# Layer 1 of a two-layer gated attention kernel: a list of units with counts per step, and turns by block transposes and DMAs

## The chip, the core and the metric

The kernel runs on one core of one Trainium2 chip. The metric is the device time of one launch in microseconds. A core has TensorE (matmuls; PE in the profile), VectorE (DVE), ScalarE (ACT), GpSimd (POOL) and SyncE (SP), which here issues nearly all DMAs; all engines run at the same time and wait for each other by semaphores. SBUF holds 128 partitions; PSUM has eight banks of 128 x 512 float32.

## The reference

The input is 16 batches of 128 tokens of width 512, with 128 context rows of width 128 per batch. Two layers each do attention to the context and a feed-forward part, both behind a layer norm and added through a tanh gate. All is float32. Layer 0 has attention with 16 heads through latents of width 64, and a feed-forward part with two of eight low-rank adapters per token. The change is in layer 1:

```python
# attention, 16 heads of 32
qp = q @ Wq.T                                   # q = layernorm(x)
k, v = jnp.split(latent_kv @ Wkv_expand.T, 2, axis=-1)
scores = jnp.einsum('bhqd,bhkd->bhqk', qh, kh) * inv_sqrt_d   # causal
attn = jax.nn.softmax(scores, axis=-1)
out = jnp.einsum('bhqk,bhkd->bhqd', attn, vh) ... @ Wout.T
# feed-forward: a mixture of 8 low-rank maps per token
h = relu(x @ W1 + b1)
alpha = softmax(h @ W2 + b2)                    # 8 shares per token
vx = jnp.einsum('krd,bsd->bskr', V, x)
out = jnp.einsum('bsk,bskd->bsd', alpha, jnp.einsum('kdr,bskr->bskd', U, vx))
```

## The kernel before

The 16 batches form four groups of four (`GB = 4`, `GT = 512` tokens). Projections run over the tokens of a whole group, attention over one batch. TensorE contracts over partitions, so the normalised rows (tokens on partitions) have to be turned (features on partitions) before a product. The kernel turns in two ways. `turned` (L1164) lets TensorE transpose four 128 x 128 blocks into PSUM, and `drain` (L1158) copies them out on VectorE or ScalarE. `standard` (L1198) has VectorE transpose 32 x 32 blocks in place, and `turn_all` (L1192) moves the blocks with 16 DMAs on SyncE, each of 32 partitions.

In layer 1, group `g` and batch `b` go through these steps:

- `load_latents`, `latents` (L1172, L1176): load the context of a group, turn it on TensorE through a "tr" PSUM tile, drain it to `kvT`, and start the next group's load. `keys(g, c)` (L1185) makes four tiles of keys.
- `standard`, `tokens` (L1218): normalise and turn a group's rows; `queries(g, c)` (L1222) makes four tiles of queries.
- `score(b)` (L1235): values and scores of a batch (two PSUM pools), then the softmax on VectorE, ScalarE and GpSimd, and block transposes into the only buffer `eb` (L1261). `carry(b)` (L1265) moves the lower blocks with ten DMAs to `late[:, 0]` or `eT_even`. `values(b)` (L1271) and `project(b)` (L1284) finish the attention; the residual and its moments run on VectorE.
- `ffn_normal`, `ffn_tokens` (L1300, L1312): normalise a group for the feed-forward part into `late[:, 1]` and turn it on TensorE. `hidden(g, c)`, `share_parts(g)`, `shares(g)` (L1318, L1334, L1347) make the shares of the eight maps and send them through DRAM to `late[:, 2]` or `late[:, 3]` by 4 and 8 DMAs. `ranks(g, c)` and `mixture(b)` (L1377, L1387) make the output, and `store` (L1400) sends it.

Tiles come from pools. The tag "xn" of `lnp` has two buffers for rows of 512; the tag "xnT" has one for a turned group; the tag "tr" has two PSUM banks, "mm" four and "acc" two. A new tile waits until the last reader of a buffer is done.

The order of work is set in two ways. On TensorE and SyncE the layer's instructions stay in program order (L164 to L177, `keep_in_program_order`). On VectorE, ScalarE and GpSimd a planner orders them at build time by its own estimates, with the program order as priority. At run time each engine goes through its own list in order.

The main loop (L1531) runs over steps `s` from 2 to 17. It does the values and projection of batch `b = s - 2` and the scores of batch `s`. Between them, `take` (L1436) pulls units from the list `fill`. Each entry has a step from which it may run and a cost (16 for most), and a running debt `owed` decides how many units a call pulls. `near[0]` tells `drain` to use VectorE only, right behind a score. Layer 0's last down products are mixed with the first queries, keys and scores ahead of the loop (L1500 to L1530).

Of the kernel before, what the change touches and what calls it, by code (L numbers as in the profile page):

```python
# [42 lines left out]
def kernel(  # L43
# [1132 lines left out]
    def latents(g):  # L1176
        tr = tr_tile(f"kv1tr_{g}")
        for i in range(GB):
            transpose(tr[:, ts(i, P)], kv[g][:, i, :], ident)
        kvT[g] = le.tile([P, GT], F32, tag="kvT", name=f"kv1T_{g}")  # L1180
        drain(kvT[g], tr)
        if g + 1 < NG:
            load_latents(g + 1)
# [34 lines left out]
    def tokens(g, xb):  # L1218
        xa[g] = lnp.tile([P, ND, GT], F32, tag="xnT", name=f"xnT_a1_{g}", bufs=1)
        turn_all(xa[g].rearrange("p c (i t) -> p (c i) t", i=GB), xb)  # L1220

    def queries(g, c):  # L1222
        q_ps = tr_tile(f"q1_ps{g}_{c}")
        for d in range(ND):
            matmul(
                q_ps, aqo_sb[:, d, ts(c, P)], xa[g][:, d, :],
                start=(d == 0), stop=(d == ND - 1),
            )
        q_c = le.tile([P, GT], F32, tag=f"q{c}", name=f"q1_{g}_{c}")
        drain(q_c, q_ps)  # L1230
        qs.setdefault(g, []).append(q_c)
# [68 lines left out]
    def ffn_normal(g):  # L1300
# [3 lines left out]
        nc.vector.reciprocal(rstdf[:, bs], rstdf[:, bs])  # L1304
        for i in range(GB):
            b = g * GB + i
            nc.vector.tensor_scalar(
                late[:, 1, 4 * i : 4 * i + 4].rearrange("p c t -> p (c t)"), xt[b],
                mvf[:, b, 0:1], rstdf[:, b : b + 1], ALU.subtract, ALU.mult,
            )  # L1310

    def ffn_tokens(g):  # L1312
        xf[g] = ap.tile([P, ND, GT], F32, tag="xf", name=f"xf_{g}", bufs=1)
        for i in range(GB):
            turned("f1", g * GB + i, late[:, 1, 4 * i : 4 * i + 4].rearrange(
                "p c t -> p (c t)"), xf[g])
# [30 lines left out]
    def shares(g):  # L1347
# [23 lines left out]
        avT[g] = late[:, 2 + g % 2].rearrange("p (c i) t -> p c i t", c=ND)  # L1371
# [5 lines left out]
    def ranks(g, c):  # L1377
        v_ps = (tr_tile if g < NG - 1 else mm_tile)(f"vx_ps{g}_{c}")
# [28 lines left out]
    def next_queries(g):  # L1407
        for c in range(ND):
            yield 16, lambda c=c: queries(g, c)

    def hiddens(g):
        for c in range(ND):
            yield 16, lambda c=c: hidden(g, c)
        yield 2, lambda: share_parts(g)

    def all_ranks(g):
        for c in range(ND):
            yield 16, lambda c=c: ranks(g, c)

    def mixtures(g, start, end):  # L1420
        for i in range(start, end):
            yield 16, lambda i=i: mixture(g * GB + i)

    def at(step, units):
        return [(step, n, u) for n, u in units]

    fill = at(AHEAD, next_queries(1)) + at(4.5, next_queries(2))
    fill += at(6, hiddens(0)) + at(7.5, next_queries(3))
    fill += at(8.5, all_ranks(0)) + at(8.5, mixtures(0, 0, 2))
    fill += at(10.5, hiddens(1)) + at(10.5, mixtures(0, 2, 4)) + at(11, all_ranks(1))  # L1430
    fill += at(11, mixtures(1, 0, 2))
    fill += at(14.5, hiddens(2)) + at(15, mixtures(1, 2, 4)) + at(16, all_ranks(2))
    fill += at(17, mixtures(2, 0, 1)) + at(NB + AHEAD, mixtures(2, 1, 2))
    owed = [0]

    def take(step, cost):  # L1436
        owed[0] += cost
        while owed[0] > 0:
            if not fill or fill[0][0] > step:
                owed[0] = 0  # L1440
                break
            _, n, unit = fill.pop(0)
            unit()
            owed[0] -= n
# [58 lines left out]
    for n in range(1, 3):  # L1503
        down(q, n)
    for c in range(ND):
        if c == 2:
            latents(0)
# [22 lines left out]
    standard(late[:, 1], 2, mv1, rstd1, "a1")  # L1530
    for s in range(AHEAD, NB + AHEAD):  # L1531
        b = s - AHEAD
        first, second, third = (0, 18, 14) if s < GB + AHEAD else (14, 28, 20)
        if b > GB and b % GB == 0:
            first, second = first + 16, second - 16
        values(b)
        settle()
        turn = s < NB and s % GB == 0
        if turn:
            latents(s // GB)  # L1540
        take(s, first)
        if turn:
            for c in range(ND):
                keys(s // GB, c)
            owed[0] -= 17
        if b > 0 and b % GB == 0:
            ffn_tokens(b // GB - 1)
            owed[0] -= 12
        if s == 6:
            standard(late[:, 1], 3, mv1, rstd1, "a1")  # L1550
            tokens(3, late[:, 1])
        if s < NB:
            score(s)
            near[0] = True
        settle()
        take(s + 0.5, second)
        near[0] = False
        project(b)
        settle()
        take(s + 0.5, third)  # L1560
# [4 lines left out]
        if s == 3:  # L1565
            tokens(2, late[:, 1])
# [5 lines left out]
    owed[0] = 0  # L1572
    take(NB + AHEAD, 1000)
    ffn_tokens(NG - 1)
    for _, unit in hiddens(NG - 1):
        unit()
    mixture((NG - 2) * GB + 2)
    store(1)
    settle()
    for _, unit in all_ranks(NG - 1):  # L1580
        unit()
    for g in (NG - 2, NG - 1):
        for _, unit in mixtures(g, 3 * (NG - 1 - g), 4):
            unit()
            store(1)
# [72 lines left out]
```

## Time and profile before

| what | value |
|---|---|
| median of 3 runs (range) | 1540.49 us (1539.66 to 1541.77) |
| the profiled execution | 1540.21 us |
| its span, first to last instruction | 1538.4 us |
| TensorE busy, mean granted clock | 1491.5 us, 0.995 |
| VectorE, ScalarE, GpSimd busy | 838.9, 431.5, 436.5 us |
| first values of layer 1 start | 1168.80 us |
| values of batch 4 start | 1234.17 us |
| last mixture ends | 1534.56 us |

A page of the profile gives each engine's busy time, the longest chain of waits, and groups of instructions by line. In a group's row, the names stand as output <- inputs, then the shape, the count, the busy time, the mean of one in ns, the idle time before it and what ended it. Rows in order of time begin with the start and the length in us; a bracket at the end is the idle time of that engine before it and the instruction that ended it. `q_ps` is a query product, `xtr_f` a TensorE transpose for the feed-forward part, `kv1tr` one of the context, `SPq` SyncE's queue of DMAs. A row of a stretch gives its start and end, its length, and then the busy time of each engine with its count of instructions, the granted clock, the share of the DMA engines and GB/s.

### The profile page before, as it was taken

The page shows a single profiled execution, that of the slowest core. Times are in us where ns is not written, and L with a number is a line of the kernel's source. Part 1 is how long each engine was busy: PE and PEld are TensorE (multiplying, and loading weights), DVE is VectorE, ACT ScalarE, POOL GpSimd, SP SyncE. Part 2 cuts the span into 40 slices and gives each one's busy share as a digit, 9 for nine tenths or more (in the row PEclk, how much of TensorE's full clock was granted, in tenths as well). Part 3 has the DMA queues.
Part 4 walks back from the last instruction along what each step waited for, and adds up shares of the span by engine and source line. Part 5 has one row for each costly group of instructions (what it writes and reads, how often), then busy time and mean ns, then how long its engine had stood idle before and what let it go on. Part 6 is the DMA issues. An engine that isn't in the chain of part 4 may idle for free.

```text
span 1538.4 us, 19401 instructions
## 1 busy us (share of the span) xinstructions
PE 1491.5 (97%) x6768; PEld 1003.4 (65%) x6768; DVE 838.9 (55%) x1727; ACT 431.5 (28%) x1423; POOL 436.5 (28%) x437
## 2 busy tenths in 40 slices
PE   7999999999999999999999999999999899999998
PEld 5667778878876666876687667766766344444444
DVE  3264654555465556565575556455657775666422
ACT  2252433343240222022101221022124553545210
POOL 2052633642531233113321332033222221221100
PEclk9999999999999999999999999999999999999999
DMA  9335567444536721632245124521544542233402
GB/s 308 108 76 90 144 178 172 100 114 89 107 59 155 238 70 57 162 122 72 72 127 141 70 72 134 149 78 48 140 101 109 82 68 57 31 69 56 89 14 69
DMA packets 372017, 161.39 MB, mean 105 GB/s; under 512 B 299344, under 2 KB 347216, under 8 KB 369744
## 3 DMA queue, kind: packets, MB, share of 16 engines
q1 hardware_dynamic: 370624, 158.44, 41.1%
q10 hardware_dynamic: 1296, 1.71, 0.3%
q8 instruction: 54, 0.88, 0.2%
q14 instruction: 43, 0.35, 0.1%
HBM read 106.35 MB, written 18.09 MB: 81 GB/s over the span
## 4 chain that ended last, share of the span: by engine, by line
PE 86%; DVE 5%; SPq 3%; DMA 2%; ACT 1%; issue 1%; POOL 1%; DVEq 0%; ACTq 0%; POOLq 0%
PE y_ps L165 14%; PE fy_ps L165 12%; PE q_ps L165 10%; PE t_ps L165 7%; PE l_ps L165 7%; PE hs_ps L165 7%; PE ht_ps L165 5%; PE c_ps L165 4%; PE vx_ps L165 3%; PE h_ps L165 3%; PE my_ps L165 3%; PE s_ps L165 3%; SPq L175 3%; PE k_ps L165 2%; ACT e L190 1%
## 5 line engine op out<-in xcount | busy, mean ns | idle before, releaser
L1080 POOL TENSOR_TENSOR near<-base,a 128x512 f32<-128x512 f32 x32 | 41.6, 1301 | 349.4 <-ACT base L1077 208.0
L197 POOL TENSOR_TENSOR e<-e,rden_a 128x512 f32<-128x512 f32 x64 | 66.5, 1039 | 243.6 <-DVE rden_a L195 240.9
L647 POOL TENSOR_TENSOR e<-e,rden_a 128x512 f32<-128x512 f32 x64 | 66.1, 1039 | 190.3 <-DVE rden_a L645 190.3
L1077 ACT ACTIVATE a<-a 128x512 f32<-128x512 f32 x64 | 40.3, 630 | 276.9 <-DVE a L1076 276.8
L165 PE MATMUL q_ps<-xnT_a,fq 128*128 128x256 f32 (+1 forms) x448 | 117.2, 414 | 0.7 <-ACT xnT_a L87 0.7
L165 PE MATMUL l_ps<-t,b_sb 128*128 128x512 f32 x256 | 115.2, 592 | 1.4 <-DVE t L1015 1.4
L640 ACT ACTIVATE e<-s_ps,nmx_a 128x128 f32<-128x128 f32 x256 | 90.7, 387 | 85.9 <-DVE nmx_a L629 38.5
L190 ACT ACTIVATE e<-e,nmx_a 128x128 f32<-128x128 f32 x256 | 98.8, 387 | 32.9 <-DVE nmx_a L185 32.8
L1076 DVE TENSOR_TENSOR a<-l_ps,base 128x512 f32<-128x512 f32 x64 | 44.1, 688 | 110.9 <-PE l_ps L165 110.8
L165 PEld LDWEIGHTS q_ps<-xnT_a,fq 128*128 128x128 f32 x448 | 85.8, 192 | 26.3 <-issue 11.5
L1142 DVE SCALAR_TENSOR_TENSOR x<-fy_ps,gw,x 128x256 f32<-128x256 f32 x112 | 46.5, 476 | 84.8 <-PE fy_ps L165 84.8
L165 PEld LDWEIGHTS l_ps<-t,b_sb 128*128 128x128 f32 x256 | 48.6, 190 | 61.7 <-issue 58.1
L165 PE MATMUL fy_ps<-ring,far 128*128 128x256 f32 x384 | 87.2, 380 | 0.0
L714 DVE SCALAR_TENSOR_TENSOR x<-y_ps,gates,x 128x256 f32<-128x256 f32 x112 | 48.8, 477 | 70.4 <-PE y_ps L165 70.3
L165 PE MATMUL y_ps<-fo_raw,c 128*128 128x256 f32 x384 | 85.7, 380 | 0.0
L165 PEld LDWEIGHTS fy_ps<-ring,far 128*128 128x128 f32 x384 | 72.6, 190 | 12.4 <-issue 2.5
L165 PEld LDWEIGHTS y_ps<-fo_raw,c 128*128 128x128 f32 x384 | 72.4, 190 | 10.1 <-ACT c L87 0.5
L165 PE MATMUL ht_ps<-T,ring 128*128 128x256 f32 x256 | 65.7, 379 | 0.0
L165 PE MATMUL t_ps<-a,a_sb 128*128 128x512 f32 x128 | 65.4, 592 | 0.0
L165 PE MATMUL t_ps<-base,a_sb 128*128 128x512 f32 x128 | 65.4, 592 | 0.0
L165 PE MATMUL c_ps<-eT,kvr 128*128 128x512 f32 x128 | 60.8, 620 | 3.0 <-DMA chosen<-rows 3.0
L165 PEld LDWEIGHTS hs_ps<-xnT_f,ring 128*128 128x128 f32 x256 | 48.4, 190 | 22.7 <-issue 14.8
(241 smaller groups left out, 2934.8 us busy)
## 6 DMA issues: line engine op xcount, KB each, us to landing
ring<-w SPq DMA_DIRECT2D x32, 896.0 KB, 4.5
eT<-eb SPq DMA_DIRECT2D x336, 64.0 KB, 2.3
ring<-w SPq DMA_DIRECT2D x16, 1024.0 KB, 5.8
ring<-in_f_w SPq DMA_DIRECT2D x12, 1024.0 KB, 5.3
late<-eb SPq DMA_DIRECT2D x80, 64.0 KB, 2.3
wq<-in_wq SPq DMA_DIRECT2D x8, 512.0 KB, 5.4
quarters<-in_f_w SPq DMA_DIRECT2D x32, 128.0 KB, 2.7
w<-sums SPq DMA_DIRECT2D x8, 512.0 KB, 3.4
```

The costliest lines, as they stand in the source:

```text
L165: ins = nc.tensor.matmul(*args, **kw)
L175: ins = nc.sync.dma_start(out=dst, in_=src)
L190: nc.scalar.activation(dst[:, ts(i, P)], src[:, ts(i, P)], AF.Exp, bias=nmx[:, i : i + 1], accum_out=den[:, i : i + 1],)
L197: nc.gpsimd.tensor_tensor(d3, d3, rden.unsqueeze(2).to_broadcast([P, 4, P]), ALU.mult)
L640: nc.scalar.activation(e[:, ts(i, P)], s_ps[:, ts(i, P)], AF.Exp, bias=nmx[:, i : i + 1], accum_out=den[:, i : i + 1],)
L647: nc.gpsimd.tensor_tensor(e3, e3, rden.unsqueeze(2).to_broadcast([P, 4, P]), ALU.mult)
L714: pin(nc.vector.scalar_tensor_tensor(dst, y_ps, gate_x[0], dst, ALU.mult, ALU.add))
L1076: nc.vector.tensor_tensor(a, l_ps, base, ALU.add)
L1077: nc.scalar.activation(a, a, AF.Gelu_apprx_tanh)
L1080: nc.gpsimd.tensor_tensor(mix, base, second, ALU.add)
L1142: nc.vector.scalar_tensor_tensor(dst, y_ps[:, ts(i, half)], q.first[:, t : t + 1], dst, ALU.mult, ALU.add,)
```

## The change

The units of layer 1 are now a plain list, and a table gives the counts that each step takes: ahead of the values, behind them, behind the scores and behind the projection. The latents are turned by one VectorE block transpose and 16 DMAs, at other places in the program: group 0 between the down products 1 and 2, the others at the end of steps 2, 6 and 10. The feed-forward tokens of groups 1 and 2 are turned by `standard` and `turn_all` in place of TensorE. The turned tokens of group 2 lie in the feed-forward part's buffer "xf", and their sends come ahead of the loop; group 3 is normalised into `late[:, 3]` at the end of step 3 (before: `late[:, 1]` at step 6). The queries of group 1 lie in `late[:, 2]`. The shares of even groups now go to `late[:, 3]`, those of odd ones to `late[:, 2]`. Ranks of group 2 use "mm" PSUM tiles.

```diff
     def latents(g):
-        tr = tr_tile(f"kv1tr_{g}")
-        for i in range(GB):
-            transpose(tr[:, ts(i, P)], kv[g][:, i, :], ident)
+        mine = lnp.tile([P, GT], F32, tag="xn", name=f"kvb_{g}")
+        nc.vector.transpose(mine, kv[g].rearrange("p i d -> p (i d)"))
+        mine = mine.rearrange("p (i d) -> p i d", d=P)
         kvT[g] = le.tile([P, GT], F32, tag="kvT", name=f"kv1T_{g}")
-        drain(kvT[g], tr)
+        whole = kvT[g].rearrange("p (i t) -> p i t", t=P)
+        for t in range(NK):
+            for k in range(NK):
+                send(whole[ts(k, BK), :, ts(t, BK)], mine[ts(t, BK), :, ts(k, BK)])
...
     def tokens(g, xb):
-        xa[g] = lnp.tile([P, ND, GT], F32, tag="xnT", name=f"xnT_a1_{g}", bufs=1)
+        if g == 2:
+            xa[g] = ap.tile([P, ND, GT], F32, tag="xf", name="xnT_a1_2", bufs=1)
+        else:
+            xa[g] = lnp.tile([P, ND, GT], F32, tag="xnT", name=f"xnT_a1_{g}", bufs=1)
...
+        if g == 1:
+            q_c = late[:, 2, 4 * c : 4 * c + 4].rearrange("p c t -> p (c t)")
...
     def ffn_normal(g):
...
+        if 0 < g < NG - 1:
+            standard(late[:, 1], g, mvf, rstdf, "f1")
+            return
...
     def ffn_tokens(g):
         xf[g] = ap.tile([P, ND, GT], F32, tag="xf", name=f"xf_{g}", bufs=1)
+        if 0 < g < NG - 1:
+            turn_all(xf[g].rearrange("p c (i t) -> p (c i) t", i=GB), late[:, 1])
+            return
...
-        avT[g] = late[:, 2 + g % 2].rearrange("p (c i) t -> p c i t", c=ND)
+        avT[g] = late[:, 3 - g % 2].rearrange("p (c i) t -> p c i t", c=ND)
...
-        v_ps = (tr_tile if g < NG - 1 else mm_tile)(f"vx_ps{g}_{c}")
+        v_ps = (tr_tile if g < NG - 2 else mm_tile)(f"vx_ps{g}_{c}")
...
+    fill = units(queries, 1) + units(queries, 2) + units(queries, 3, (0, 1))
+    fill += units(hidden, 0) + units(queries, 3, (2,)) + one(share_parts, 0)
+    fill += units(queries, 3, (3,))
+    for g in range(NG - 1):
+        fill += units(ranks, g)
+        if g == NG - 2:
+            break
+        fill += one(ffn_tokens, g + 1) + mixtures(g, (0, 1))
+        fill += units(hidden, g + 1) + one(share_parts, g + 1) + mixtures(g, (2, 3))
+    plan = {
+        2: (1, 0, 1, 1), 3: (1, 0, 1, 0), 4: (0, 0, 1, 1), 5: (0, 0, 1, 1), 6: (0, 1, 1, 1),
+        7: (0, 2, 2, 0), 8: (0, 0, 1, 0), 9: (0, 1, 1, 1), 10: (0, 1, 2, 1),
+        11: (0, 0, 2, 2), 12: (0, 1, 1, 1), 13: (0, 1, 1, 1), 14: (0, 1, 2, 1),
+        15: (0, 0, 2, 2), 16: (0, 1, 1, 0), 17: (0, 0, 1, 4),
+    }
...
-    for n in range(1, 3):
-        down(q, n)
+    down(q, 1)
+    latents(0)
+    down(q, 2)
     for c in range(ND):
-        if c == 2:
-            latents(0)
         queries(0, c)
...
     standard(late[:, 1], 2, mv1, rstd1, "a1")
+    tokens(2, late[:, 1])
     for s in range(AHEAD, NB + AHEAD):
         b = s - AHEAD
...
+        ahead, first, second, third = plan[s]
+        take(ahead)
         values(b)
         settle()
...
+        take(first)
+        if s < NB and s % GB == 0:
             for c in range(ND):
                 keys(s // GB, c)
...
+            settle()
+        if b == GB:
+            ffn_tokens(0)
         if s < NB:
             score(s)
             near[0] = True
+        take(second)
+        near[0] = False
         settle()
...
         project(b)
-        settle()
-        take(s + 0.5, third)
+        take(third)
...
         if s == 3:
-            tokens(2, late[:, 1])
+            standard(late[:, 3], 3, mv1, rstd1, "a1")
+            tokens(3, late[:, 3])
+        if s % GB == 2 and s // GB + 1 < NG:
+            latents(s // GB + 1)
         if b % GB == GB - 1:
             ffn_normal(b // GB)
         if s < NB:
             carry(s)
         store(2)
...
+    g = NG - 1
+    ffn_tokens(g)
+    mixture((g - 1) * GB)
+    for unit in units(hidden, g):
         unit()
-    mixture((NG - 2) * GB + 2)
+    mixture((g - 1) * GB + 1)
+    share_parts(g)
+    mixture((g - 1) * GB + 2)
+    settle()
     store(1)
```

More of the change, by code (lines that the diff above doesn't have):

```diff
@@ L1228, in queries @@
             )
-        q_c = le.tile([P, GT], F32, tag=f"q{c}", name=f"q1_{g}_{c}")
+        if g == 1:
+            q_c = late[:, 2, 4 * c : 4 * c + 4].rearrange("p c t -> p (c t)")
+        else:
+            q_c = le.tile([P, GT], F32, tag=f"q{c}", name=f"q1_{g}_{c}")
         drain(q_c, q_ps)
@@ L1403, in store, with units, mixtures, one @@
             send(out[b], xt[b])
[L1407 to L1444, printed above, removed]
+    def units(what, g, ns=range(ND)):
+        return [lambda n=n: what(g, n) for n in ns]
+    def mixtures(g, ns):
+        return [lambda n=n: mixture(g * GB + n) for n in ns]
+    def one(what, g):
+        return [lambda: what(g)]
+    fill = units(queries, 1) + units(queries, 2) + units(queries, 3, (0, 1))
[8 more added lines that the diff above has]
+    plan = {
[4 rows of a table added]
+    }
+    def take(n):
+        for _ in range(n):
+            fill.pop(0)()
     q = first
@@ L1530 @@
     standard(late[:, 1], 2, mv1, rstd1, "a1")
+    tokens(2, late[:, 1])
     for s in range(AHEAD, NB + AHEAD):
         b = s - AHEAD
-        first, second, third = (0, 18, 14) if s < GB + AHEAD else (14, 28, 20)
-        if b > GB and b % GB == 0:
-            first, second = first + 16, second - 16
+        ahead, first, second, third = plan[s]
+        take(ahead)
         values(b)
         settle()
[L1538 to L1542, printed above, removed]
+        take(first)
+        if s < NB and s % GB == 0:
             for c in range(ND):
                 keys(s // GB, c)
[L1545 to L1551, printed above, removed]
+            settle()
+        if b == GB:
+            ffn_tokens(0)
         if s < NB:
@@ L1554 @@
             near[0] = True
+        take(second)
+        near[0] = False
         settle()
-        take(s + 0.5, second)
-        near[0] = False
         project(b)
-        settle()
-        take(s + 0.5, third)
+        take(third)
         if s == AHEAD:
@@ L1571 @@
         store(2)
[L1572 to L1575, printed above, removed]
+    g = NG - 1
+    ffn_tokens(g)
+    mixture((g - 1) * GB)
+    for unit in units(hidden, g):
         unit()
-    mixture((NG - 2) * GB + 2)
+    mixture((g - 1) * GB + 1)
+    share_parts(g)
+    mixture((g - 1) * GB + 2)
+    settle()
     store(1)
-    settle()
-    for _, unit in all_ranks(NG - 1):
+    for unit in units(ranks, g):
         unit()
[L1582 to L1585, printed above, removed]
+    for b in range(g * GB - 1, NB):
+        mixture(b)
+        store(1)
     store(0)
```

## The prediction

> **What bounds the kernel.** I read the page's busy shares first, then the span cut into stretches around layer 1, the groups of transposes, and then the engines in order of time: TensorE for its gaps, SyncE's queue for its sends, VectorE for the step that feeds them.
>
> ```profile
> PE 1491.5 (97%) x6768; PEld 1003.4 (65%) x6768; DVE 838.9 (55%) x1727; ACT 431.5 (28%) x1423; POOL 436.5 (28%) x437
> 1123.30:1168.50 45.20, 45.12 (x236) 34.03 (x236) 20.25 (x44) 16.74 (x70) 10.06 (x9) 1.00 0.35 68
> 1183.90:1220.50 36.60, 30.10 (x185) 14.14 (x185) 25.47 (x54) 18.35 (x74) 8.99 (x9) 0.95 0.71 157
> 1320.00:1400.00 80.00, 77.62 (x439) 37.31 (x439) 49.48 (x102) 37.10 (x148) 16.12 (x16) 1.00 0.30 54
> ```
>
> TensorE sets the time; in the stretches (length, then busy PE, PEld, DVE, ACT, POOL, clock, DMA) it is idle mainly between 1183.9 and 1220.5, where the clock also falls to 0.95.
>
> ```profile
> L170 PE MATMUL xtr_f<-ident,late 128*128 128x128 f32 x64 | 9.1, 280 | 6.0 <-DVE late L1307 3.0 <-ACT xf L87 1.4 <-DVE q L85 1.3
> L170 PE MATMUL kv1tr<-ident,kv 128*128 128x128 f32 x16 | 2.6, 285 | 0.9 <-DVE q L85 0.9
> L175 SPq DMA_DIRECT2D chosen<-rows x16: 324/428/1168, 474.4 to 964.9; - x16
> ```
>
> ```profile
> 1183.96 1.08 PE L165 MATMUL o_ps<-late,v 128*32 128x128 f32 x32 [1.42 <-DMA late<-eb]
> 1202.08 3.70 PE L165 MATMUL k_ps<-kv1T,akv_sb 128*128 128x512 f32 x8 [1.09 <-ACT kv1T L87]
> 1211.74 5.40 PE L165 MATMUL q_ps<-xnT_a,aqo_sb 128*128 128x512 f32 x8 [3.26 <-DMA xnT_a<-late]
> ...
> 1459.86 3.70 PE L165 MATMUL vx_ps<-xf,mw_sb 128*128 128x512 f32 x8 [2.38 <-DVE late L1385]
> ```
>
> ```profile
> 1175.10 6.66 SPq L175 DMA_DIRECT2D late<-eb  x10
> 1181.86 0.56 SPq L175 DMA_DIRECT2D mw_sb<-in_m_w  x1
> ...
> 1190.59 7.14 SPq L175 DMA_DIRECT2D eT<-eb  x10
> 1198.13 11.87 SPq L175 DMA_DIRECT2D xnT_a<-late  x16
> 1210.10 6.66 SPq L175 DMA_DIRECT2D late<-eb  x10
> ```
>
> SyncE issues its sends in program order, about 0.67 us each. From 1175 to 1217 it is the engine that TensorE waits for: a batch's values wait for its carry (ten sends), a group's queries for its tokens (sixteen).
>
> **The change, by stretch.** Units: a filler (queries, hidden, ranks, mixture, project) is 3.5 us (two of them, 16 matmuls, in 6.97); keys 3.5 and 0.4 for their drain; score 2.2; values 1.0. A carry is 6.7 us of sends and usable 2.2 later (last ends 1181.76, values start 1183.96); tokens are 11.2 (the four groups took 10.71 to 11.87) and usable 1.75 later (1210.00 to 1211.74).
>
> *Up to the first values (1168.80).* Removed: group 0's four transposes with their gap, 1122.5 to 1123.9, 1.4 us, so TensorE comes to the keys at 1129.4. Added: a VectorE transpose and 16 sends. The turned block needs an "xn" buffer; both are held by group 1's rows until 1117.7, the next two rows take them until 1121.8, so it ends at 1122.5. The trace has no such send. Bounds: 0.44 each (the 12 KB router rows, four in 1.75) and 0.70 (64 KB). This one carries 16 KB in 128 runs, nearest to the router's 96: I take 0.47, 7.5 in all, usable at about 1132.0 (at 0.70: 1135.8; if a buffer is free earlier, no wait). The keys started at 1130.74: **+1.3** (-1.4 to +5.1). The down weights queued behind these sends (1115.25 before, about 1130 now) are not read before 1153; the move costs nothing while those 18 us last.
>
> *First values to the values of batch 4 (1168.80 to 1234.17: 65.4 before).* Time 0 is now the query unit ahead of the first values. TensorE: unit, values, score 2, unit, project, unit: 17.2. Unit, values, score 3: 23.9, and group 2's first query. SyncE: batch 1's blocks stay where VectorE has them (behind group 2's rows, ready at 6.3), carry 1 to 13.1, three weight loads to 14.8, then what is moved forward: tokens of group 2 to 26.2, latents of group 1 to 33.7, their load 0.5, and only then carry 2, to 40.9. In the kernel before, carry 2 stood ahead of the tokens. The query waits 23.9 to 27.95, 4.0 us. Then carry 2, usable at 43.1, finds TensorE at 36.7 (query with its slow clock 5.3, project 3.5): 6.4 more.
>
> The clock has to be added. The row: after 3.26 us idle the same eight matmuls took 5.40, not 3.60, while gaps of 2.38 and 1.62 were followed by the usual 3.70 or less. The Trainium skill ("TensorE: Matmul & The Clock Gate", Part 1) says that an idle window of about 3.4 us halves the clock until as long a busy one; its windows run free. By it a full window at half speed costs 1.7; by the row 1.8. By the rule's threshold alone my two waits cost it twice and the late waits of 2.5 never; by the row the threshold can be as low as 3.3, which changes neither. Without the clock this stretch would be 3.5 shorter. I count 1.8 and 1.7.
>
> So 43.1 + 1.7 + values 1.0 + keys 3.9 + score 2.2 + three units 10.5 = 62.4. Tokens of group 3 and carry 3 follow on SyncE (40.9, 52.1, 58.8); their rows need VectorE by 40.9 and may be 2 late: 63.0. Then values, score, three units: 76.7. Carry 4 goes out 16.5 after its score (1208.5 to 1225.0 before), usable at 77.3. Two units more are done than before at that point, so 70.3, with the 0.6 of late rows 70.9: **+5.5** (+2 to +9; with sends at 0.70, +9.2).
>
> *From there to the last mixture (1234.17 to 1534.56).* Removed: the ffn transposes of groups 1 and 2 with their drains, 3.15 (1326.71 to 1329.86) and 4.2 (1405.7 to 1409.92); two latents, 1.0; the ranks' waits of 1.16 and 2.38, as ranks 2 get the four idle score banks and ranks 1 start a step after their shares; 1.7 of the 2.4 before the last hidden units (gaps of 1.30, 0.22 and 0.88 from 1478.5 on), as ranks 2 and a mixture now stand around the last group's transposes: 13.6. Added: shares 0 stand right behind their parts, so the drain is bare: 1.2 (0.9 to 3). Their 12 sends stay ahead of carry 7, and it was usable 19.5 after the shares (10.6 + 6.7 + 2.2); TensorE now has 17.6 until those values: 1.9. The ffn tokens now go through SyncE behind carry 9: carry 9 leaves 13.8 after its score and ends at 20.5, 16 sends to 31.7, usable at 33.45; TensorE reaches the hidden units at 30.9 (ranks, project, ranks, values, ranks, score, mixture, project, mixture, values, score): 2.55, and once more for group 2: 5.1. VectorE gets 3.4 us more per group (four 0.7 transposes and slower rows, less two drains) in a step where it already works 10.5 of 17 (49.5 of 80 above); exposed 2.0 (0 to 4). Sum 10.2: **-3.4** (-12 to +3). The drain of latents (0.69) and their new VectorE transpose (0.69) cancel, beside TensorE. Lent buffers cost nothing: the ffn buffer is empty until group 0's tokens, after the last query of group 2, and the late quarter until the shares of group 1.
>
> Total: +1.3 + 5.5 - 3.4 = +3.4. The profiled execution took 1540.21 with a span of 1538.4, 1.8 outside it; the median of the runs is 0.3 above it. Span 1541.8, runs **1544**.
>
> **Rivals.** (A) The forecast, 1544, own range 1540 to 1550. For it: sends in program order, each row measured. Against: the order on VectorE is the planner's, not the program's.
>
> (B) Latents cost as much per send as the 64 KB ones, 0.70. Then the keys start 3.8 later and carry 2 another 3.7: 1551.5. For it: the sends of shares into the late tile, with half as many runs as a 64 KB one, cost 0.62 too. Against: the router rows.
>
> (C) Faster, by one mechanism: VectorE turns batch 1 before group 2's rows.
>
> ```profile
> 1161.88 0.84 DVE L1142 SCALAR_TENSOR_TENSOR x<-fy_ps,gw,x 128x256 f32<-128x256 f32 x2
> 1168.48 0.71 DVE L1207 STREAM_TRANSPOSE late<-xn_a 128x512 f32<-128x512 f32 x1 [5.75 <-PE fy_ps L165]
> ...
> 1172.59 2.44 DVE L1261 STREAM_TRANSPOSE eb<-e 128x512 f32<-128x512 f32 x4
> ```
>
> It idles 5.75 us with batch 1 ready at 1163.1, waiting for the weights' room. Turned first, carry 1 ends at 3.4, tokens of group 2 land at 18.2, unwaited for, carry 2 is held only by its own softmax (18.6 after the score, usable at 34.2, TensorE there at 30.9), and batch 4's values come at 61.5: -3.9 in place of +5.5, 1534.5. It decides if the first of these turns starts before the last down product ends. Against it: nothing changes the priorities of the two.
>
> (D) The late turns are hidden: SyncE is free for ffn tokens when ranks 0 end because carry 9 leaves over 5 us earlier, and shares 0 drain at once. Then the 10.2 added vanish: 1533.7. Against: score to carry was 12.2 to 13.8 throughout.
>
> (E) The change does nothing for TensorE, its transposes being pulled under waits: 48 transposes lie on its chain, so I give it nothing of its own.
>
> **How the numbers follow.** A 0.42, B 0.24, C 0.16, D 0.12, the rest unforeseen. A measurement of this kernel tells about 0.2% (3.1 us) from no change: slower above 1543.6, faster below 1537.4. Slower: six tenths of A, all of B, most of the rest, 0.54. Same: the rest of A, 0.18 with a little of C. Faster: C and D, 0.28. The range goes from C and D, which the 1.4 of an early buffer extends, to B with VectorE's 4 and a wait or two more: 1532 to 1558.
>
> **What would show it.** TensorE waits before group 2's first query (about 4) and before values 2 (about 6), each with a dip of the clock; carry 2 some 30 us behind carry 1 on SyncE, not 15; latents' sends near 0.45; the keys' start near 1132; 2 to 3 us before the first hidden units of groups 1 and 2; no wait at ranks. Wrong if carry 1 goes out before the last down product ends, if latents' sends cost 0.7, or if VectorE's new order delays scores.

## The result and the profile after

The changed kernel takes 1555.43 us (median of 4 runs, 1552.56 to 1555.63). The kernel before, run beside it, takes 1540.31 (1539.66 to 1541.77). The ratio is 1.009, with a 95% interval of 1.0077 to 1.0103: the change costs 0.9%. The profiled execution took 1555.62 with a span of 1553.8, 15.4 longer than the span before. TensorE's mean clock fell from 0.995 to 0.984.

The page's busy times and three stretches of layer 1 (start and end, length, busy PE, PEld, DVE, ACT, POOL, clock, DMA share, GB/s):

```profile
PE 1492.2 (96%) x6720; PEld 1004.6 (65%) x6720; DVE 843.7 (54%) x1733; ACT 428.6 (28%) x1417; POOL 436.2 (28%) x437
1123.30:1139.50 16.20, 12.30 (x24) 5.17 (x25) 2.65 (x5) 1.17 (x2) 0.00 (x0) 0.89 0.46 110
1183.00:1226.00 43.00, 24.52 (x110) 10.93 (x108) 25.02 (x53) 17.15 (x70) 8.31 (x8) 0.78 0.68 139
1336.60:1421.70 85.10, 83.36 (x465) 39.52 (x464) 59.40 (x121) 36.09 (x146) 16.63 (x16) 0.98 0.41 68
```

TensorE issues 48 matmuls fewer, yet it is busy for as long as before. The stretch around group 2's queries and the values of batch 2 has become the hole: 24.5 us of work in 43 us, at a clock of 0.78.

TensorE in order of time, at five of its six longest waits in layer 1 (the bracket is the wait ahead and what ended it; the sixth, 1.99, stands ahead of the values at 1316.35):

```profile
1134.33 5.37 PE L165 MATMUL k_ps<-kv1T,akv_sb 128*128 128x512 f32 x8 [3.81 <-DMA kv1T<-kvb]
1209.13 6.15 PE L165 MATMUL q_ps<-xnT_a,aqo_sb 128*128 128x512 f32 x8 [11.20 <-DMA kv1T<-kvb]
1226.63 1.93 PE L165 MATMUL o_ps<-eT,v 128*32 128x128 f32 x32 [7.91 <-DMA eT<-eb]
1228.49 5.03 PE L165 MATMUL k_ps<-kv1T,akv_sb 128*128 128x512 f32 x8
...
1357.17 8.80 PE L165 MATMUL h_ps<-xf,mw_sb 128*128 128x512 f32 x16 [1.74 <-DMA kv1T<-kvb]
...
1439.46 8.78 PE L165 MATMUL h_ps<-xf,mw_sb 128*128 128x512 f32 x16 [6.96 <-DMA xf<-late]
```

The name in the second bracket is misleading. The query product reads no latents; the profile names an event of the same queue at the same time. What it needs are group 2's tokens, `xnT_a<-late`. SyncE's queue in the same time shows it:

```profile
1122.33 10.24 SPq L175 DMA_DIRECT2D kv1T<-kvb  x16
...
1133.86 13.88 SPq L175 DMA_DIRECT2D xnT_a<-xb_a  x16
...
1181.06 6.66 SPq L175 DMA_DIRECT2D late<-eb  x10
1188.13 0.37 SPq L175 DMA_DIRECT2D mw_sb<-in_m_w  x1
1188.55 0.50 SPq L175 DMA_DIRECT2D mw_sb<-in_m_vT  x1
1189.09 0.51 SPq L175 DMA_DIRECT2D mw_sb<-in_m_uT  x1
1189.64 17.59 SPq L175 DMA_DIRECT2D xnT_a<-late  x16
1207.33 10.25 SPq L175 DMA_DIRECT2D kv1T<-kvb  x16
1217.63 0.59 SPq L175 DMA_DIRECT2D kv<-in_kvc  x1
1218.33 6.66 SPq L175 DMA_DIRECT2D eT<-eb  x10
```

Two things differ from what a reader of the profile before would expect. The latents' sixteen sends take 10.25, 0.64 each, and not 7.5. The tokens' sixteen sends take 17.59, and not 11.2: they are issued right behind three 1 MB loads (without these ahead of them they take 12.05, in the first experiment). The first six hold the queue for 10.84, up to 1200.5; the last load, issued at 1189.09, landed 11.6 later; the other ten sends take 6.70, the usual 0.67 each. No row of this list starts before the one ahead of it is done, so carry 2 (the last row) leaves 37 us after carry 1; before it was 15.

Where the 15.3 us lie (the marks are the query unit ahead of the first values, the values of batch 4 and the end of the last mixture; after, two query units more are done by the second mark, 7.0 us):

| stretch | before | after | difference | predicted |
|---|---|---|---|---|
| to the first values (after: to the unit ahead of them) | 1168.80 | 1174.07 | +5.3 | +1.3 |
| to the values of batch 4 | 65.4 | 85.5 - 7.0 | +13.1 | +5.5 |
| to the end of the last mixture | 300.4 | 290.3 + 7.0 | -3.1 | -3.4 |

### The profile page after: what moved, and what is told of

Its sections match the earlier page's. It is cut to its first block, busy times and chain, and to the rows that moved or that the text cites. A ratio compares the mean times of both kernels' runs of the same rounds, so it can differ in the third digit from the quotient of the medians.

```text
span 1553.8 us, 19423 instructions
## 1 busy us (share of the span) xinstructions
PE 1492.2 (96%) x6720; PEld 1004.6 (65%) x6720; DVE 843.7 (54%) x1733; ACT 428.6 (28%) x1417; POOL 436.2 (28%) x437
## 4 chain that ended last, share of the span: by engine, by line
PE 84%; SPq 5%; DVE 4%; DMA 3%; ACT 2%; issue 1%; POOL 1%; DVEq 0%; ACTq 0%; POOLq 0%
PE y_ps L165 14%; PE fy_ps L165 12%; PE q_ps L165 9%; PE l_ps L165 7%; PE t_ps L165 7%; PE hs_ps L165 7%; PE ht_ps L165 5%; SPq L175 5%; PE h_ps L165 4%; PE c_ps L165 4%; PE vx_ps L165 3%; PE my_ps L165 3%; PE k_ps L165 3%; PE s_ps L165 3%; ACT e L190 1%
## 5 line engine op out<-in xcount | busy, mean ns | idle before, releaser
L197 POOL TENSOR_TENSOR e<-e,rden_a 128x512 f32<-128x512 f32 x64 | 66.5, 1039 | 247.5 <-DVE rden_a L195 247.3
L165 PEld LDWEIGHTS y_ps<-fo_raw,c 128*128 128x128 f32 x384 | 72.4, 190 | 10.1 <-ACT c L87 0.5
L165 PE MATMUL q_ps<-xnT_a,aqo_sb 128*128 128x512 f32 x128 | 60.3, 620 | 12.2 <-DMA kv1T<-kvb 11.2
L165 PE MATMUL h_ps<-xf,mw_sb 128*128 128x512 f32 x128 | 60.0, 624 | 8.7 <-DMA xf<-late 7.0
L165 PE MATMUL t_ps<-a,a_sb 128*128 128x512 f32 x128 | 65.4, 592 | 0.0
L165 PE MATMUL t_ps<-base,a_sb 128*128 128x512 f32 x128 | 65.4, 592 | 0.0
```

The source lines that it names most:

```text
L165: ins = nc.tensor.matmul(*args, **kw)
L197: nc.gpsimd.tensor_tensor(d3, d3, rden.unsqueeze(2).to_broadcast([P, 4, P]), ALU.mult)
```

## The experiments

My theory after the result: the loss is SyncE's queue in the first steps of layer 1. Sends that stood nowhere (the latents') or later (group 2's tokens) now stand ahead of carry 2, and the weight loads make them longer. Rivals to it: the late feed-forward turns, the weight loads alone, and the table of counts itself. Every ratio below is to the kernel before, run on the same chip; 0.1% is 1.5 us.

### The weight loads behind carry 2

```diff
-    for n, w in enumerate((m_w1, m_vT, m_uT)):
-        send(mw_sb[...], w...)
...
         if s < NB:
             carry(s)
+        if s == AHEAD:
+            for n, w in enumerate((m_w1, m_vT, m_uT)):
+                send(mw_sb[...], w...)
```

> The changed kernel, with the three 1 MB weight loads sent behind carry 2 (end of step 2) and no longer ahead of group 2's tokens. Theory (SyncE's queue is the path, and those loads fill it and the DMA engines): the 16 token sends take 11.2 us as in the other groups, not 17.6, and start 1.7 earlier; the wait of 11.2 before group 2's first query falls to about 3, its dip of the clock goes, and the time falls by 6 to 9 us from 1555.4, to about 1548. Rival (the sends are slow because so many small ones are in flight): the 16 sends still take 16 to 18 us and the time stays within 2 us of 1555.

Measured: ratio 1.0106 (1.0088 to 1.0123), no gain over 1.009. The sends got short, as the theory had it, but the time did not fall. The edit did what it should at its own place, and gave all of it back one group further on. SyncE's queue of this kernel, then TensorE's waits:

```profile
1187.22 12.05 SPq L175 DMA_DIRECT2D xnT_a<-late  x16
1199.37 10.24 SPq L175 DMA_DIRECT2D kv1T<-kvb  x16
...
1218.88 19.03 SPq L175 DMA_DIRECT2D xnT_a<-late  x16
1238.02 6.66 SPq L175 DMA_DIRECT2D late<-eb  x10
```

```profile
1201.37 5.37 PE L165 MATMUL q_ps<-xnT_a,aqo_sb 128*128 128x512 f32 x8 [4.35 <-DVE e L1266]
1218.69 1.93 PE L165 MATMUL o_ps<-eT,v 128*32 128x128 f32 x32 [8.52 <-DMA eT<-eb]
1246.63 1.94 PE L165 MATMUL o_ps<-late,v 128*32 128x128 f32 x32 [9.28 <-DMA late<-eb]
```

Group 2's tokens now take 12.05 and the query wait falls from 11.20 to 4.35. But the loads stand ahead of group 3's tokens, which take 19.03 in their turn and hold carry 3, and the values of batch 3 wait 9.28 where they had not waited. So the cost of the loads is that of whatever block sends come next, and behind those stood a carry in both places.

### The latents by TensorE, at the new places

```diff
     def latents(g):
-        mine = lnp.tile([P, GT], F32, tag="xn", name=f"kvb_{g}")
-        nc.vector.transpose(mine, kv[g].rearrange("p i d -> p (i d)"))
...
+        tr = tr_tile(f"kv1tr_{g}")
+        for i in range(GB):
+            transpose(tr[:, ts(i, P)], kv[g][:, i, :], ident)
         kvT[g] = le.tile([P, GT], F32, tag="kvT", name=f"kv1T_{g}")
-        ... 16 sends
+        drain(kvT[g], tr)
```

> The changed kernel, with the latents of all four groups turned by TensorE as before, at the new places in the program. Theory (the latents' 16 sends of 0.64 stand on the path in the prelude and ahead of carry 2): the keys of group 0 start at about 1131 in place of 1134.3 at full clock (5.3 us back up to the first values), carry 2 leaves 10.8 earlier and values 2 wait 0 in place of 7.9 and 1.7 of clock; less the 2 us of four times four transposes. Time about 1541, the query's wait of 11.2 unchanged. Rival (the path is only the tokens behind the weight loads): about 1550.

Measured: 1.0058 (1.0043 to 1.0073), a gain of about 5 us and not of 15; the time is near the rival's. But the wait at the values of batch 2 is gone, so the latents' sends made it. And group 0's transposes now stand between two down products, where TensorE waits:

```profile
1114.42 1.09 PE L170 MATMUL kv1tr<-ident,kv 128*128 128x128 f32 x4 [6.39 <-DVE xn_a L1204]
1115.30 5.76 PE L165 MATMUL fy_ps<-ring,far 128*128 128x256 f32 x16
...
1212.12 5.19 PE L165 MATMUL q_ps<-xnT_a,aqo_sb 128*128 128x512 f32 x8 [9.73 <-DMA xnT_a<-late]
```

The new place suits a turn that TensorE does not do; for TensorE it is 6.4 us too early, with a slow product behind it. The weight loads still lengthen group 2's tokens, to 18.44. So this run gives only a lower bound on what the latents' sends cost.

### The feed-forward tokens by TensorE, where the list has them

```diff
     def ffn_normal(g):
-        if 0 < g < NG - 1:
+        if g in ():
             standard(late[:, 1], g, mvf, rstdf, "f1")
             return
     def ffn_tokens(g):
-        if 0 < g < NG - 1:
+        if g in ():
             turn_all(...)
```

> The changed kernel, with the feed-forward tokens of groups 1 and 2 turned by TensorE as before, at their places in the new list. Theory: the waits of 1.7 and 7.0 before the hidden units and 1.8 of slow clock behind each (12.2 in all) go; 2 x 1.9 of transposes and 2 x 1.2 of drains come back; 1549 to 1550. Rival (VectorE's longer list holds the carries, and its relief moves more): below 1546. Rival (DMA turns cost nothing net): 1555.

Measured: 1.0124 (1.0109 to 1.0139), slower still. The two waits at hidden units are gone, and in their place the transposes wait 3.91 twice (and 0.33 and 0.79) for their drains:

```profile
1350.52 1.12 PE L170 MATMUL xtr_f<-ident,late 128*128 128x128 f32 x4 [3.91 <-DVE xf L1160]
```

The list has these tokens right behind a score, where `drain` uses VectorE alone, and VectorE is then busy with that score's softmax. So the list's place was made for the sends. That is not all of its loss. The profile is 8.8 longer than that of the kernel after, and 4.0 of this stand already at the first queries of layer 1 (1119.32 against 1115.36), ahead of all that the edit touches; what shifted them is not known. The run says nothing against TensorE at another place; that is tried below.

### The kernel before with the latents' part of the change alone

```diff
     def latents(g):
-        tr = tr_tile(f"kv1tr_{g}")
...
+        nc.vector.transpose(mine, kv[g].rearrange("p i d -> p (i d)"))
+        ... 16 sends
...
-    for n in range(1, 3):
-        down(q, n)
+    down(q, 1)
+    latents(0)
+    down(q, 2)
...
+        if s % GB == 2 and s // GB + 1 < NG:
+            latents(s // GB + 1)
```

> The kernel before, with one part of the change alone: the latents by a VectorE block transpose and 16 sends, at the new places. Theory: up to the first values +5.3 as in the changed kernel; carry 2 leaves 10.8 later and the tokens of group 2 after it too, so values 2 and group 2's first query each wait several us more, 6 to 10 together with the clock; the two later latents save 1 to 2. 1550 to 1556. Rival (it is the new order of tokens and counts that costs): 1541 to 1546, the prelude alone.

Measured: 1.0085 (1.0069 to 1.0102), in the theory's range. This one part of the change, the sends with their new places, brings nearly the whole loss to the kernel before, with its own order of tokens, its own list and its own feed-forward turns. Its queue and its two longest waits:

```profile
1188.94 16.61 SPq L175 DMA_DIRECT2D kv1T<-kvb  x16
1205.60 0.59 SPq L175 DMA_DIRECT2D kv<-in_kvc  x1
1206.31 6.66 SPq L175 DMA_DIRECT2D eT<-eb  x10
```

```profile
1135.33 3.67 PE L165 MATMUL k_ps<-kv1T,akv_sb 128*128 128x512 f32 x8 [3.80 <-DMA kv1T<-kvb]
1214.61 1.94 PE L165 MATMUL o_ps<-eT,v 128*32 128x128 f32 x32 [11.60 <-DMA eT<-eb]
```

Here it is the latents that stand behind the weight loads and take 16.61, and carry 2 behind them that makes the values wait 11.60. In the kernel after it is the tokens that stand behind the loads, and the latents behind the tokens; the loss is about the same.

### The kernel before with the weight loads behind carry 4

```diff
-    for n, w in enumerate((m_w1, m_vT, m_uT)):
-        send(mw_sb[...], w...)
...
             carry(s)
+        if s == 4:
+            for n, w in enumerate((m_w1, m_vT, m_uT)):
+                send(mw_sb[...], w...)
```

> The kernel before, with the three 1 MB loads of the mixture's weights moved from behind carry 1 to behind carry 4. Theory: the loads hurt only the block sends that follow at once on SyncE (11.5 to 17.6 us for the sixteen of group 2 in the kernel after); in the kernel before carry 2 stood between and took 7.14 instead of 6.66, so here they cost about 2 us of SyncE and half of that in the query wait of 3.26: 1540 to 1543 on this chip, where before is about 1542. Rival: the loads slow the start of layer 1 in either kernel: 1537 or less.

Measured: 0.9997 (0.9989 to 1.0006), no difference. In the kernel before, these loads cost nothing that can be measured, as carry 2 needs batch 2's softmax and leaves well after them. In these runs they cost something only where block sends stand right behind them.

### The kernel after with TensorE's latents at the old places

```diff
-    down(q, 1)
-    latents(0)
-    down(q, 2)
+    for n in range(1, 3):
+        down(q, n)
     for c in range(ND):
+        if c == 2:
+            latents(0)
         queries(0, c)
...
         values(b)
         settle()
+        if s < NB and s % GB == 0:
+            latents(s // GB)
...
-        if s % GB == 2 and s // GB + 1 < NG:
-            latents(s // GB + 1)
```

> The kernel after, with the latents turned by TensorE at the places of the kernel before (group 0 between the second and third query tile, the others behind the values). Theory: the latents' sends and their places are most of the loss; what is left is the query wait behind the weight loads (about 10 instead of 3.3 with a slow clock) and two late hidden units, less the transposes saved: 1543 to 1547, first values within 1 us of those before, no wait at values 2. Rival (the table of counts and the list are the loss, as the run with TensorE's latents at the new places stayed at 1551.5): 1550 or more.

Measured: 1.0061 (1.0042 to 1.008), not better than at the new places and outside what my theory allowed. The time is the rival's, but its cause, the table of counts and the list, is not borne out: the next run keeps both and gains 0.5%. As expected, the first values come early (1171.49, the unit ahead included) and those of batch 2 do not wait. But the query wait is 11.15, and the keys of group 1 wait:

```profile
1202.98 5.53 PE L165 MATMUL q_ps<-xnT_a,aqo_sb 128*128 128x512 f32 x8 [11.15 <-DMA xnT_a<-late]
1216.98 5.37 PE L165 MATMUL k_ps<-kv1T,akv_sb 128*128 128x512 f32 x8 [3.45 <-DVE kv1T L85]
```

With the latents out of the way, the tokens' sends behind the weight loads (18.22 in this run) are enough to lose 11 us. The keys' wait is one that I had not foreseen.

### The same, and the weight loads behind carry 4

The edit is that of the run two above, on this kernel.

> As the last one, and the three weight loads behind carry 4, where no group's tokens follow. Theory: the sixteen sends of group 2 take 11.5 to 12, the query wait falls to 3 to 5, no other wait rises: 1537 to 1541, at or below the kernel before. Rival (the wait only moves, as when the loads stood behind carry 2): within 1.5 of the last run, with values 5 or the queries of group 3 waiting instead.

Measured: 1.001 (1.000 to 1.002), 0.5% less than the run before it.

```profile
1183.52 11.91 SPq L175 DMA_DIRECT2D xnT_a<-late  x16
```

```profile
1197.51 5.07 PE L165 MATMUL q_ps<-xnT_a,aqo_sb 128*128 128x512 f32 x8 [3.29 <-issue]
1211.66 6.53 PE L165 MATMUL k_ps<-kv1T,akv_sb 128*128 128x512 f32 x8 [4.05 <-DVE kv1T L85]
```

The tokens take 11.91 and the query waits 3.29. The time ends a little above my range, 0.1% from the kernel before; the keys of group 1 still wait. Moving the loads, worth nothing in the kernel before and nothing behind carry 2, is worth half a per cent here: the next sends (carry 5) leave 7.9 us behind the last load, and the values that need them do not wait.

### The rows of the feed-forward part behind the carry

```diff
-        if b % GB == GB - 1:
-            ffn_normal(b // GB)
         if s < NB:
             carry(s)
+        if b % GB == GB - 1:
+            ffn_normal(b // GB)
```

> As the last one, and the rows of the feed-forward part (groups 1 and 2) stand behind the carry of their step in program order, so that the planner gives VectorE's block transposes of the softmax the higher priority. Theory: group 2's hidden units waited 6.96 because VectorE made the rows before it turned batch 13 and so held carry 13, on which SyncE's sends of the tokens stand in line; now carry 13 leaves about 13 after its score and the wait is 2 to 3: 3 to 5 us below the last run. Rival: the rows themselves are then late and the sends wait for them instead: the wait stays 5 or more, time within 1 of the last run or above.

Measured: 1.0009 (0.9998 to 1.002), no change. The edit did not do what it was for: from 1300 to 1440, where both groups' rows are made, VectorE's instructions stand in the same order in the profiles of this run and of the one before it. So it tests neither the theory nor the rival. In the kernel after, VectorE made group 2's rows from 1412.87 to 1419.5 and turned batch 13 behind most of them, so that carry 13 left at 1419.02, 17.4 after its score, and the hidden units waited 6.96. In these two runs batch 13 is turned behind the first two rows, carry 13 leaves 14.6 after its score, and the wait is 4.09 and 3.89.

### The feed-forward tokens by TensorE, ahead of the scores

On the kernel with TensorE's latents at the old places and the loads behind carry 4, without the edit to the rows:

```diff
-        fill += one(ffn_tokens, g + 1) + mixtures(g, (0, 1))
+        fill += mixtures(g, (0, 1))
...
-        10: (0, 1, 2, 1)
+        10: (0, 1, 1, 1)
-        14: (0, 1, 2, 1)
+        14: (0, 1, 1, 1)
...
-        if b == GB:
-            ffn_tokens(0)
+        if b > 0 and b % GB == 0:
+            ffn_tokens(b // GB - 1)
         if s < NB:
             score(s)
```

> The kernel after with TensorE's latents at the old places and the weight loads behind carry 4, and with the feed-forward tokens of groups 1 and 2 turned by TensorE ahead of the scores of steps 10 and 14, as in the kernel before. Theory: the block transposes and sends of these tokens cost 2.4 and 4.1 of waiting and about 1.6 and 2.6 of slow clock at the hidden units, 10.7 in all, against some 7.3 for the transposes and their drains: 2 to 4 us below the same kernel with sent tokens (about 1539 to 1541.5), no wait over 1 at these hidden units. Rival: the drains come late, as where the transposes stood right behind a score (8.9 of waits): 1544 or more.

Measured: 0.9979 (0.9966 to 0.9991), faster than the kernel before and some 4.8 us (0.31%) below the same kernel with sent tokens, a little more than my theory allowed. No wait over 0.6 us is left at these transposes or hidden units. So the sent feed-forward tokens cost more than the transposes that they replace, even with the latents' sends and the weight loads out of their way.

### Group 3's rows and sends behind carry 4

```diff
-        if s == 3:
-            standard(late[:, 3], 3, mv1, rstd1, "a1")
-            tokens(3, late[:, 3])
...
             carry(s)
+        if s == 4:
+            standard(late[:, 3], 3, mv1, rstd1, "a1")
+            tokens(3, late[:, 3])
+        if s == 3:
+            ... the weight loads
```

> As the last one, with the rows and sends of group 3's tokens moved from step 3 to behind carry 4, and the weight loads behind carry 3. Theory: the keys of group 1 waited 4 to 6, with a slow clock of 1.5 to 3, because VectorE made group 3's rows and batch 3's softmax before it drained the latents; with the rows gone from step 3 that wait is near the 1.1 of the kernel before: 3 to 6 us below the last run, at or under 1537, faster than the kernel before. Rival: the queries of group 3 or carry 5 come late instead: within 1.5 of the last run or above.

Measured: 1.0044 (1.0027 to 1.0061), 10 us slower than the run before: my theory fell twice. The keys of group 1 still wait 5.44, so group 3's rows did not cause that wait. And the queries of group 3 now wait 11.44 for their tokens, which leave behind carry 4 at 1237.94:

```profile
1250.73 6.39 PE L165 MATMUL q_ps<-xnT_a,aqo_sb 128*128 128x512 f32 x8 [11.44 <-DMA xnT_a<-late]
```

The moved step of the change (group 3 at step 3) is thus a gain and not a loss with this list.

What does hold the keys is seen on VectorE in the kernel of the run before (`kv1T` is the drained tile):

```profile
1208.19 2.49 DVE L1268 STREAM_TRANSPOSE eb<-e 128x512 f32<-128x512 f32 x4 [0.19 <-issue]
1210.60 0.66 DVE L85 COPY kv1T<-kv1tr 128x512 f32<-128x512 f32 x1
```

The transposes of the latents start at 1207.21 and are done before 1208; their drain waits for batch 3's turn of 2.49. `drain` alternates between VectorE and ScalarE by a plain flip, and in this kernel the flip falls on VectorE; in the kernel before it fell on ScalarE.

### The drain of group 1's latents on ScalarE

```diff
-        drain(kvT[g], tr)
+        if g == 1:
+            flip[0] ^= 1
+            nc.scalar.copy(kvT[g], tr)
+        else:
+            drain(kvT[g], tr)
```

> The kernel that beat the one before (TensorE's latents at the old places, weight loads behind carry 4, the feed-forward tokens by TensorE ahead of the scores), with one edit: the drain of group 1's latents is given to ScalarE, which is idle there (from 1207.7 to 1213.8 in the profile of the same order with sent tokens), and not to VectorE, where it stands behind the 2.49 of batch 3's block transposes. Theory: the keys' wait of 3.45 falls to about 1 and their 5.40 of slow clock to 3.6 or 3.7: 3 to 4.5 us below the last such run, a ratio to the kernel before of 0.995 to 0.996. Rival: the keys are held by something else that ends at the same time (the moved rows of group 3 gave no gain either): within 1 of that run, ratio 0.9975 to 0.9985.

Measured: 1532.67, ratio 0.9948 (0.9934 to 0.9961), half a per cent faster than the kernel before and some 4.8 us below the last such run, a little more than my theory. TensorE around the place:

```profile
1194.45 3.67 PE L165 MATMUL q_ps<-xnT_a,aqo_sb 128*128 128x512 f32 x8 [3.16 <-issue]
...
1201.48 1.08 PE L165 MATMUL o_ps<-eT,v 128*32 128x128 f32 x32
1202.49 0.66 PE L170 MATMUL kv1tr<-ident,kv 128*128 128x128 f32 x4
1203.95 3.70 PE L165 MATMUL k_ps<-kv1T,akv_sb 128*128 128x512 f32 x8 [0.80 <-ACT kv1T L1183]
```

The wait falls from 3.45 to 0.80 and the slow keys from 5.40 to 3.70, 4.35 in all. The query in the first row, which the edit does not touch, took 6.34 behind a wait of 3.31 in the profile of the run without it and 3.67 behind 3.16 here, so the two profiles differ by more than the edit. The values of batch 4 come 66.5 us after the query unit ahead of the first values, less two units 59.5, against 65.4 before and 78.5 after. This kernel has one thing that neither of those two has, the loads behind carry 4, and gives group 1's drain to ScalarE by hand. What remains of the change in it is the list with its counts, group 2's tokens sent forward, group 3's at step 3, the lent buffers and the ranks' banks. Which of these brings the half per cent, no run separates.

### The sends by their shape

At the end of the kernel before, 52 sends that compute nothing:

```diff
     store(0)
+    src, dst = late[:, 1], late[:, 2]
+    for t in range(NK):
+        for k in range(NK):
+            send(dst[ts(k, BK), 0:4, ts(t, BK)], src[ts(t, BK), 0:4, ts(k, BK)])
...
+            send(dst[ts(k, BK), :, ts(t, BK)], src[ts(t, BK), :, ts(k, BK)])
...
+            send(dst[ts(k, BK), t], src[ts(t, BK), k])
...
+        send(dst[:, 0:4, ts(t, BK)], src[:, 0:4, ts(t, BK)])
```

> The kernel before with 52 extra sends on SyncE behind its last store, from the late tile to itself (they only add time at the end): sixteen of 32 partitions x 4 x 32 values (the latents' shape, 16 KB), sixteen of 32 x 16 x 32 (the tokens' shape, 64 KB), sixteen of 32 x 128 contiguous values (16 KB), four of 128 x 4 x 32 (64 KB). Theory (an issue costs by the number of its runs of memory): 0.6, 0.67, about 0.4, 0.67. Rival (a send from SBUF to SBUF costs 0.6 or more whatever its shape, and the router rows are cheap because they go to DRAM): 0.6 for the third as well.

Measured, SyncE's queue, one row for each of the four shapes:

```profile
1538.30 10.31 SPq L175 DMA_DIRECT2D late<-late  x16
1548.71 10.69 SPq L175 DMA_DIRECT2D late<-late  x16
1559.50 10.07 SPq L175 DMA_DIRECT2D late<-late  x16
1571.07 2.73 SPq L175 DMA_DIRECT2D late<-late  x4
```

That is 0.64 for 16 KB in 128 runs, 0.67 for 64 KB in 512, 0.63 for 16 KB in 32 runs, and 0.68 for 64 KB over 128 partitions. The rival's 0.6 holds: for these four shapes from SBUF to SBUF the issue costs nearly the same. A quarter of both bytes and runs (first row against second) saves 0.03 us, a quarter of the runs at equal bytes (third against first) 0.01. That the router rows are cheap because they go to DRAM is not tested by it.

## Why the prediction was right or wrong

The side was right: slower was given the highest chance, and 1555.4 lies inside the range, though near its upper end and outside the 1540 to 1550 of forecast A itself. The likeliest time, 1544, was 11 us too low, and the terms that were mis-sized are these.

**Up to the first values, +1.3 predicted, +5.3 measured.** VectorE's transpose of the latents ended at 1122.3, as worked out (1122.5). The step that failed is the price of a send: "nearest to the router's 96: I take 0.47". It was 0.64, nearer to rival B's 0.70, and 2.7 us longer in all. I had compared by the number of runs, and the extra sends show that this hardly matters. The row to take was the one of the same kind, block sends from SBUF to SBUF (0.67). What makes the router's rows cheaper stays open. The keys then waited 3.81, and the 1.8 us of slow clock that I counted elsewhere I had not counted here. Together with the 1.3 that makes 5.8, against 5.3 measured.

**First values to batch 4, +5.5 predicted, +13.1 measured.** The mechanism was right to the row: group 2's query waits, then the values of batch 2, each with a dip of the clock, with carry 2 behind tokens and latents on SyncE. The failed step is "tokens of group 2 to 26.2": sixteen sends at 0.70 behind three loads at 0.5. With time 0 at the unit ahead, they began at 15.6 (14.8 predicted) and ended at 33.2. From there on the chain adds up as worked out: latents and the next load to 44.2 (11.0 instead of 8.0), carry 2 usable at 52.6 instead of 43.1. The later start, the tokens and the latents, 0.8 + 6.2 + 3.0, less some 0.5 for a shorter landing, are the 9.5 us by which the values of batch 2 came late. From there to batch 4 it took 33.0 instead of 34.8. I had costed an issue behind loads by one that stood in a free queue. In layer 1 of the kernel before no block send followed such loads directly. But layer 0 has a row that shows the effect, and I overlooked it (`selT<-chosen`, 32 DMAs of 96 KB; behind the count the shortest, median and longest issue in ns):

```profile
L175 SPq DMA_DIRECT2D selT<-chosen x32: 302/437/7908, 485.6 to 971.6; - x32
```

The longest, 7.91 us, is the first of eight that stand right behind 3 MB of loads at 485.55. These eight took 14.00; the next eight, behind one load of 1 MB, took 4.42. In the kernel after it shows twice: the tokens of group 1 stand behind one ring load of 1 MB and took 13.88, those of group 2 behind three and took 17.59. While the loads were under way (the DMA engines' share is 1.11 in the records from 1190 to 1200), the first of group 2's sends took 11.4 us from issue to landing; those issued once the last load had landed took about 2.3. The Trainium skill ("DMA: Bandwidth & Descriptors", Queues, rings and completion order) says that each DMA engine takes the descriptors of a queue in order. That fits the late landing. Why the issue itself is held as well, no run here shows.

**From there to the end, -3.4 predicted, -3.1 measured.** The sum was right by luck, from parts that were not. The hidden units of groups 1 and 2 were to wait 2.55 each. They waited 1.74 and 6.96, and each pair ran in 8.8 and not 7.0: 12.2 in all, against the 5.1 counted and 2.0 for VectorE. The batch of values ahead of the shares' sends waited 1.99 (1.9 predicted) and the shares' drain 1.73 (1.2). On the other side TensorE's work fell more than I had found in single rows. In this stretch it was busy 287.5 before; after, 259.6 + 17.3 for the last mixtures + 7.0 for the two units, 283.9, and some 5.3 of that is slow clock. Idle time was 12.9 before and 13.4 after. The waits at the ranks are gone, as predicted.

**The clock.** I took the threshold from the row of 3.26 us and gave waits of 2.5 no cost. The runs here show slow products behind waits from 1.74 up (8.80 for 7.03), and a full clock behind 3.80, 3.38 and 3.16 (3.67 for eight matmuls each time). Behind 2.13, in the run with the loads behind carry 2, the hidden units took the usual 7.11. Behind the same wait of 2.38, at the ranks of group 2, eight matmuls took 3.70 in the kernel before and 5.40 in that kernel with the latents' part. So between about 1.7 and 3.8 the length of the wait alone does not decide it; I had read three gaps as a threshold. It differs from one execution of a kernel to the next, too: the 13 with TensorE's latents at the old places and the loads behind carry 4 took 1538.77 to 1545.97, the three shortest at a mean clock of 0.991 or 0.992, the others at 0.987 to 0.990. The Trainium skill ("TensorE: Matmul & The Clock Gate", Part 1) has an idle window of about 3.4 us that runs free, so that where a wait falls would matter. The full clock behind 3.80 fits that. The slow product behind 1.74 does not, as so short a wait holds no whole window; it stays unexplained.

**The rivals.** B was nearer in its price and named 1551.5; like A, it left out what the loads do to the tokens' sends. C did not come about: VectorE turned group 2's rows (from 1173.84) before batch 1's (1178.53), as the priorities had it. D did not: the late turns were not hidden. In the kernel that sends both latents and tokens the causes are not additive. Taking the latents' sends out gave 0.3%, moving the loads alone nothing, both 0.8%. No run moves only group 2's tokens back to their old place with the latents' sends left in, so what that move costs by itself is not shown.

## What to carry to other kernels

A turn by block sends is not free because TensorE no longer does it: sixteen sends held the issuing queue for 10 to 12 us here, at 16 KB as at 64 KB, and what stands behind them in program order pays. Before a group of sends is moved forward, write down the queue as a list with durations and look for the next consumer behind it, and put large loads where no small send that is waited for follows at once. When a fix moves a wait rather than removing it, as the loads behind carry 2 did, combine it with the removal of what it collides with before it is given up: the same loads, moved to where nothing right behind them is waited for, gave half a per cent. And when an edit is meant to change the order on an engine that a planner orders, look first in the profile whether the order changed.

## What the runs showed of the hardware

- In the run with the extra sends, a send from SBUF to SBUF took 0.63 to 0.68 us to issue for 16 KB and 64 KB, for 32 and 128 partitions, for runs of 128 and 512 bytes; sends of router rows to DRAM took 0.44.
- Sixteen such sends right behind three 1 MB loads on the same queue took 16.6 to 19.0 us, and elsewhere mostly 10.1 to 12.1. In the kernel after, the excess ended when the last load had landed. The three loads themselves took only 0.37 to 0.62 each to issue.
- The clock: eight matmuls took 5.07 us behind a wait of 3.29 in one kernel and 3.67 behind 3.38 in another; behind the same wait of 2.38 they took 3.70 and 5.40; and sixteen took 8.80 behind a wait of only 1.74.
